# Layer 1's front split in two, its first part two images ahead, and new weights for the side work of two scan loops

## The chip, the core and the metric

The kernel runs on one core of a Trainium2 chip. The metric is the device time of one execution in microseconds, the median of several. Five engines work beside each other, each with its own queue of instructions that it takes in order: TensorE (PE in the profile, its weight loads PEld), VectorE (DVE), ScalarE (ACT), GpSimd (POOL) and SyncE (SP), which in this kernel issues all data transfers (DMA). An engine waits at the head of its queue until the semaphores of that instruction's producers are set.

## What is computed

Input x has 16 images of 192 channels and 32 x 32 pixels, in float32. Four residual blocks follow one another, each fed with a group norm (32 groups) of x:

```
x = x + layer0(gn(x))   # mLSTM block, projection, 3x3 conv, batch norm, leaky relu
x = x + layer1(gn(x))   # Mamba: layer norm, in_proj, causal conv of 4 taps, silu, scan, gate, out_proj, layer norm, proj
x = x + layer2(gn(x))   # depthwise 3x3 conv, batch norm, clip to 0..6
x = x + layer3(gn(x))   # SS2D: in_proj, depthwise 4x4 conv, four scans, layer norm, gate, out_proj, and a local branch
```

The scans of layers 1 and 3 take most of the time. For each of 384 channels and 16 states n, over 1024 positions t:

```
h[t] = exp(dt[t] * A[n]) * h[t-1] + dt[t] * x[t] * B[t, n]
y[t] = sum over n of C[t, n] * h[t]
```

Layer 1 runs one such scan per image, layer 3 four of them (rows, columns, and both reversed).

## The kernel before

**Scan steps.** Layers 1 and 2 run as one stage (`layer12`), layer 3 as another. The core of both is `scan_run` (L864 on). A step is one half image (512 positions) and one state n: 16 images x 2 halves x 16 states = 512 steps in layer 1, 4 times as many in layer 3. Channels lie in three groups t of 128 partitions. One step has

- on ACT three `xbt` (L889, u times B) and three `da` (L909, the decay exp), each a step ahead or more;
- on PE, for each group t, three transposes and a matmul into `xb` (L917, L920; 3 PSUM buffers), one step ahead, and four transposes that add h into the PSUM tile y (L951), two steps behind;
- on DVE three scan instructions (L933), which write h (4 buffers) from da (5 buffers) and xb;
- on POOL the multiplication of all of h by C (L940), on every fourth step a tile of diagonals (L899), and in the first half of an image a copy of the carried state (L939);
- on SP the broadcast of C's row (`cb`, 256 KB, 4 buffers, L891).

**Side work.** Everything else runs beside the scan, as Python generators that yield between small pieces. `Side.add(kind, steps, start, end)` gives a generator a window of steps. `Side.tick(now)` is called four times a step and advances each generator until the weight that it has yielded matches its share of the window:

```
share = self.totals.get(kind, self.total) * (now - start) / (end - start)
while now >= end or (task[4] < share and now >= task[5]):
```

The weight of a piece is what its `yield` gives (`yield 1.7`, L1224); `yield Wait(n)` holds a generator back by n steps, after a DMA was issued. The total of a kind is learned from its first task. Weights so place pieces within their window, and windows place the tasks. A scheduler of the framework then orders each engine's instructions: it keeps to this order by priority, but lets a later instruction go ahead where its engine would be free by the scheduler's own estimate. The scan's matmuls are tied to each other in order (`in_order`).

**Layer 1's tasks for image b.** `at` is 32 b. The windows in the kernel before, with the functions:

- `prep` (`scan_rows` L801, `scan_prep` L827): projections of x to dt, B and C, softplus for dt (L841 and L842 on ACT, L843 on DVE), transposes and u = dt * x (L854 to L860). `dbl` (L812) and its transposes (L819) give B as `bt` (L821). For the odd half at +1 to +13, for the next image's even half at +26 to +30.
- `layer1_gated` (L1055): the scan's sum y is transposed back (L987), D * x is added (L1063), and POOL multiplies it into the gate (L1064).
- `layer1_out` (L1228): out_proj and the skip, into `xt` (one buffer). `layer1_gate` (L1209): the gate's projection from `xn` and its silu, +8 to +12.5.
- `layer1_front` of image b + 1, +12.5 to +20: loads x and layer 0's result y0, applies layer 0's batch norm and leaky relu (L1156, L1157), adds (L1158), stores x1, group norm (`group_norm`, L321), normalises to `xf` (L1163), stores xf1, then layer norm (`layer_norm`, L349) into `xn`, and in_proj of the conv's half (L1176 on PE, L1180 on ACT), stored to `xin` in DRAM (L1181). x and `xn` are the same one-buffer tile `x1`.
- `layer1_conv` of image b + 1, +20 to +26: reads `xin` back as replicas shifted by tap (`replicas`, L1084; 6 buffers), four matmuls of 32 output columns for each tile (L1195), the bias (L1199), and silu of all of `xc` in one ACT instruction (L1206), with a table load before and one after it (L1207).
- `layer1_tail` of image b - 1, +13.5 to +25: layer norm, proj, x1 read again (L1259) and added (L1267), group norm, result padded to `xpad` (L1274) and stored.
- `layer2` of image b - 1, +25.5 to +34: replicas, depthwise conv on PE (`depthwise`, L1094), bias on ACT (L1293), bn_stats on DVE (L1295).

**Layer 3's tasks** have fixed windows in its 128 steps per image (L1359 on); their windows are not touched, only the weights that their pieces yield.

Of the kernel before, what the change touches and what calls it, by code (L numbers as in the profile page):

```python
# [10 lines left out]
F32 = mybir.dt.float32  # L11
# [8 lines left out]
HP = 96  # L20
DI = 384
S = 1024
# [229 lines left out]
class Program:  # L252
# [68 lines left out]
    def group_norm(self, pool, psum, x):  # L321

        nc = self.nc
        st = pool.tile([HP, 2, 2, 6], F32, name="gnst")
        mv = pool.tile([HP, 2, 2], F32, name="gnmv")
        for m in range(2):
            for i, h in enumerate(halves()):
                nc.vector.bn_stats(st[:, m, i], x[:, m, h])
            nc.vector.bn_aggr(mv[:, m], st[:, m].rearrange("p a b -> p (a b)"))
            yield 1  # L330
        ps = psum.tile([128, 512], F32, name="mm")
        nc.tensor.matmul(ps[:HP, :2], self.k("group", HP), mv[:, :, 0], start=True, stop=True)
        mean = pool.tile([HP, 2], F32, name="gnmean")
        nc.vector.tensor_copy(mean, ps[:HP, :2])
        d = pool.tile([HP, 2], F32, name="gnd")
        nc.vector.tensor_tensor(d, mv[:, :, 0], mean, SUB)
        q = pool.tile([HP, 2], F32, name="gnq")
        nc.vector.tensor_tensor(q, d, d, MUL)
        nc.vector.tensor_tensor(q, q, mv[:, :, 1], ADD)
        yield 1  # L340
        ps = psum.tile([128, 512], F32, name="mm")
        nc.tensor.matmul(ps[:HP, :2], self.k("group", HP), q, start=True, stop=True)
        r = pool.tile([HP, 2], F32, name="gnr")
        nc.vector.tensor_scalar(r, ps[:HP, :2], EPS, None, ADD)
        self.pow_mhalf(r)
        yield 1
        return mean, r, d

    def layer_norm(self, pool, psum, xs, outs, ones, p, n):  # L349

        nc = self.nc
# [3 lines left out]
        for x, o in zip(xs, outs):  # L355
            nc.vector.tensor_tensor(o, x, mean[:p, :n], SUB)
        yield len(xs)
        var = psum.tile([128, 512], F32, name="mm")
# [6 lines left out]
        for o in outs:  # L365
            nc.vector.tensor_tensor(o, o, var[:p, :n], MUL)
        yield len(xs)

# [432 lines left out]
    def scan_rows(self, seen, w_x, n, bp, dp, psum):  # L801
# [3 lines left out]
        nc = self.nc  # L805
# [8 lines left out]
        for q in range(n):  # L814
            nc.sync.dma_start(row[q], dbl[64 * q + RK + NS : 64 * q + XD])
        yield 2.6
        ps = psum.tile([128, 4, 128], F32, name="mm")
# [5 lines left out]
        )  # L823
        yield 0.5
        return dbl, row, bt

    def scan_prep(self, u, rows, q, xc, xt, new, w_dt, bp, psum):  # L827


        nc = self.nc  # L830
# [6 lines left out]
        for t in range(3):  # L837
# [5 lines left out]
            nc.vector.scalar_tensor_tensor(u.dt[:, t], e, 20.0, ps, MIN, MAX)  # L843
            yield 1
        u.ut = bp.tile([128, 4, DI], F32, name="ut")
        flat, xflat = u.ut.rearrange("p c d -> p (c d)"), xt.rearrange("p c d -> p (c d)")
        for j in range(3):
# [12 lines left out]
            nc.vector.tensor_tensor(flat[:, o], xflat[:, o], ps, MUL)  # L860
            yield 1.3 if new else 0.8
        u.ready = True
# [130 lines left out]
    def layer12(self):  # L993
        tc = self.tc
        with (
# [27 lines left out]
            for b in range(self.nb):  # L1023
                at = 2 * NS * b
                side.add("prep", prep(units[2 * b + 1]), at + 1, at + 13)
                if b:
                    side.add("gate", self.layer1_gated(units[2 * b - 1], bp, psum), at + 2, at + 3.5)
                    side.add("out", self.layer1_out(b - 1, bp, psum), at + 3.5, at + 8)
                side.add("silu", self.layer1_gate(b, bp, psum), at + 8, at + 12.5)
                if b + 1 < self.nb:  # L1030
                    side.add("front", self.layer1_front(b + 1, sp, bp, psum), at + 12.5, at + 20)
                if b:
                    side.add("tail", self.layer1_tail(b - 1, sp, bp, dp, psum), at + 13.5, at + 25)
                side.add("gate", self.layer1_gated(units[2 * b], bp, psum), at + 18, at + 21)
                if b + 1 < self.nb:
                    side.add("conv", self.layer1_conv(b + 1, bp, psum), at + 20, at + 26)
                if b:
                    side.add("layer 2", self.layer2(b - 1, bp, psum), at + 25.5, at + 34)
                if b + 1 < self.nb:
                    side.add("prep", prep(units[2 * b + 2]), at + 26, at + 30)  # L1040
            finish(self.layer1_front(0, sp, bp, psum))
            finish(self.layer1_conv(0, bp, psum))
            finish(prep(units[0]))
# [11 lines left out]
    def layer1_gated(self, u, bp, psum):  # L1055
# [4 lines left out]
        for t in range(3):  # L1060
# [3 lines left out]
            nc.gpsimd.tensor_tensor(im["sz"][:, t, h], im["sz"][:, t, h], o, MUL)  # L1064
            yield 1

# [21 lines left out]
    def depthwise(self, ps, blocks, reps, side):  # L1088

        width = W + side - 1  # L1090
        for r in range(side):
            for g, rep in enumerate(reps):
# [4 lines left out]
                )  # L1097
            yield 0.9

# [45 lines left out]
    def layer1_front(self, b, sp, bp, psum):  # L1145

        nc = self.nc
        x = bp.tile([HP, 2, S], F32, name="x1", bufs=1)
        nc.sync.dma_start(x, self.ins["x"][b].rearrange("(m p) t -> p m t", p=HP))
# [3 lines left out]
        for m in range(2):  # L1153
            for h in halves():
# [3 lines left out]
                nc.vector.tensor_tensor(x[:, m, h], x[:, m, h], v, ADD)  # L1158
                yield 0.5
        nc.sync.dma_start(self.x1[b], x)  # L1160
        mean, r, _ = yield from self.group_norm(sp, psum, x)
        for m in range(2):
            nc.vector.tensor_scalar(xf[:, m], x[:, m], mean[:, m : m + 1], r[:, m : m + 1], SUB, MUL)  # L1163
        nc.sync.dma_start(self.xf1[b], xf)
        yield 1
        xn = x
        for h in halves():
# [4 lines left out]
        for t in range(3):  # L1172
            for h in halves():
# [7 lines left out]
                nc.sync.dma_start(self.xin[b % 2][t][:, 3 + h.start : 3 + h.stop], o)  # L1181
                yield 1.7
        self.image[b]["xn"] = xn
# [44 lines left out]
    def layer1_out(self, b, bp, psum):  # L1228
# [6 lines left out]
        for h in halves():  # L1235
            for m in range(2):
# [7 lines left out]
                )  # L1244
                yield 2.6

    def layer1_tail(self, b, sp, bp, dp, psum):
# [3 lines left out]
        for h in halves():  # L1251
# [14 lines left out]
            for m in range(2):  # L1266
                nc.vector.scalar_tensor_tensor(  # L1267
                    x[:, m, h], ps[m][:HP], self.b_proj[:, m : m + 1], o[m][:HP], ADD, ADD
                )
            yield 3.4  # L1270
        nc.sync.dma_start(self.x2[b], x)
# [10 lines left out]
    def layer2(self, b, bp, psum):  # L1282
# [3 lines left out]
        for m in range(2):  # L1286
            for i in range(2):
# [5 lines left out]
                nc.scalar.activation(y2, ps[:HP], AF.Identity, bias=self.v96("2b", m))  # L1293
                yield 0.2
                nc.vector.bn_stats(self.stats[:, m, 2 * b + i], y2)  # L1295
                nc.sync.dma_start(self.y2[b, :, m, i * 512 : (i + 1) * 512], y2)
                yield 0.2

# [151 lines left out]
    def layer3_front(self, b, sp, bp, dp, psum):  # L1450
# [5 lines left out]
        for m in range(2):  # L1456
# [3 lines left out]
            for h in halves():  # L1460
# [3 lines left out]
                nc.vector.scalar_tensor_tensor(x[:, m, h], y2[:, h], 6.0, x[:, m, h], MIN, ADD)  # L1464
                yield 1
        mean, r, d = yield from self.group_norm(sp, psum, x)
# [10 lines left out]
    def layer3_local(self, b, sp, bp, psum):  # L1477
# [10 lines left out]
        for i, h in enumerate(halves()):  # L1488
            l = bp.tile([128, 3, 512], F32, name="tmp", bufs=1)[:HP]
            for m in range(2):  # L1490
# [6 lines left out]
                )  # L1497
                yield 0.2
            for m in range(2):
# [6 lines left out]
                nc.vector.tensor_tensor(x[:, m, h], x[:, m, h], ps[:HP], ADD)  # L1506
                yield 1.7
        nc.sync.dma_start(self.x3[b], x)
# [17 lines left out]
    def layer3_xc(self, b, bp, dp, psum):  # L1526
# [6 lines left out]
        def project(t):  # L1533
            for i in range(2):
# [9 lines left out]
                )  # L1544
                yield 1.7
            scratch[t] = dp.tile([128, (W + 3) ** 2], F32, name="xr")
# [4 lines left out]
        for t in range(3):  # L1551
            blocks = bp.tile([128, 16, 32], F32, name="taps", bufs=1)
            nc.sync.dma_start(blocks, self.t_conv[t])
            for i, h in enumerate(halves()):
# [7 lines left out]
                nc.vector.tensor_scalar(xc[:, t, h], ps, self.v128("3conv_b", t), None, ADD)  # L1562
                yield 0.2
        self.silu(xc)
        yield

    def layer3_tail(self, b, bp, psum):
# [4 lines left out]
        for i, h in enumerate(halves()):  # L1572
# [3 lines left out]
            yield from self.layer_norm(bp, psum, vs, vs, self.k("ones384"), 128, 512)  # L1576
            self.silu(sz)
            for t in range(3):
                nc.scalar.activation(
                    v[:, t, h], v[:, t, h], AF.Identity, bias=self.v128("3ln_b", t), scale=self.v128("3ln_g", t)  # L1580
                )
                yield 0.4
            nc.gpsimd.tensor_tensor(v[:, :, h], v[:, :, h], sz, MUL)
            yield 0.4
        for m in range(2):
            for h in halves():
# [8 lines left out]
                nc.sync.dma_start(self.out[b, m * HP : (m + 1) * HP, h], x)  # L1595
                yield 2.6

# [36 lines left out]
```

## Time and profile before

| | us |
|---|---|
| median of 4 runs | 17716.2 |
| the runs | 17702.94 to 17731.71 |
| the profiled execution | 17709.81 |
| its span | 17708.0 |
| layer 0 with what lies before it, to 4277 | 4277 |
| layers 1 and 2: first to last scan step, 4277 to 7835 | 3558 |
| between the two scan loops | 232 |
| layer 3's scan loop, 8067 to 17642 | 9575 |
| after the last scan | 66 |

The profile gives for each engine the time in which it was busy, by group of instructions (line of the kernel, engine, output <- inputs, shapes), the idle time in front of an instruction and what ended it (its releaser), and a timeline. Lines with L are lines of the kernel before. Records of PE overlap, since matmuls are pipelined; the time from one start to the next tells more than the record's length. The granted clock of TensorE was 0.98 of full speed in both scan loops.

### The profile page before, as it was taken

What the parts mean: (1) busy time and instruction counts of PE and PEld (TensorE: products, weight loads), DVE (VectorE), ACT (ScalarE), POOL (GpSimd) and SP (SyncE); (2) the same over time, 40 slices, a digit from 0 to 9 for tenths busy, and PEclk for the clock granted to TensorE, in tenths of its full rate; (3) what the DMA queues carried; (4) which work ended last, traced back from release to release, by engine and by line L of the source; (5) the groups of instructions that cost most, each with busy time, mean ns of one, the idle gap of its engine ahead of it and who ended that gap; (6) DMA issues with size and microseconds to landing.
All of it is one profiled execution on the core that took longest, in us unless ns stands there. A gap on an engine that the chain in (4) does not pass through costs nothing.

```text
span 17708.0 us, 263742 instructions
## 1 busy us (share of the span) xinstructions
PE 16110.7 (91%) x99836; PEld 11245.9 (64%) x99836; DVE 13340.8 (75%) x14875; ACT 11901.5 (67%) x19653; POOL 11462.2 (65%) x5556
## 2 busy tenths in 40 slices
PE   8999999898999999978999999999999999999998
PEld 4444444444655555546777777777777777777777
DVE  4454444454777777767888888888888888888888
ACT  2222222223766666656888888888888888888888
POOL 3333333333555555546887888788888888888888
PEclk8898888898999999989999999999999999999999
DMA  1111111112333333433333233333323332333232
GB/s 44 31 32 32 32 31 31 32 30 80 111 114 114 114 114 117 117 102 102 99 106 99 90 99 107 93 96 100 107 87 96 105 105 84 99 106 100 90 98 67
DMA packets 877951, 1511.10 MB, mean 85 GB/s; under 512 B 80336, under 2 KB 311197, under 8 KB 865834
## 3 DMA queue, kind: packets, MB, share of 16 engines
q1 hardware_dynamic: 876682, 1494.22, 28.7%
q8 instruction: 791, 12.96, 0.3%
q14 instruction: 478, 3.92, 0.1%
HBM read 1264.99 MB, written 228.92 MB: 84 GB/s over the span
## 4 chain that ended last, share of the span: by engine, by line
PE 30%; ACT 9%; DVE 8%; issue 4%; POOL 3%; DMA 0%; DVEq 0%; POOLq 0%; ACTq 0%; SPq 0%
PE y L951 8%; PE xb L917 7%; DVE h L933 6%; PE xb L920 4%; ACT da L909 3%; PE mm L1094 3%; ACT xbt L889 3%; POOL h L940 2%; PE mm L810 1%; PE mm L839 1%; PE mm L1517 1%; PE mm L1537 1%; PE mm L859 1%; PE mm L1502 1%; PE mm L1591 1%
## 5 line engine op out<-in xcount | busy, mean ns | idle before, releaser
L940 POOL TENSOR_TENSOR h<-h,cb 128x1536 f32<-128x1536 f32 x2560 | 8870.1, 3468 | 1427.5 <-DVE h L933 890.8
L909 ACT ACTIVATE da<-dt,neg_a 128x512 f32<-128x512 f32 x7680 | 5267.1, 714 | 1734.7 <-DVE h L933 1663.8
L933 DVE TENSOR_TENSOR_SCAN h<-da,carry,xb 128x512 f32<-128x512 f32 x3840 | 4653.5, 1263 | 662.7 <-PE xb L920 592.8
L951 PE MATMUL y<-const,h 128*128 128x128 f32 x30720 | 4720.6, 276 | 129.6 <-DVE ysum L1391 54.1
L933 DVE TENSOR_TENSOR_SCAN h<-da,xb 128x512 f32<-128x512 f32 x3840 | 4441.2, 1203 | 386.6 <-PE xb L920 275.4
L917 PE MATMUL xb<-const,xbt 128*128 128x128 f32 x23040 | 4081.2, 282 | 412.0 <-DVE h L933 254.0
L889 ACT ACTIVATE xbt<-ut,bt 128x384 f32<-128x384 f32 x7680 | 4174.1, 603 | 246.8 <-PE xb L917 245.0
L917 PEld LDWEIGHTS xb<-const,xbt 128*128 128x128 f32 x23040 | 2765.2, 143 | 1799.4 <-issue 639.2
L951 PEld LDWEIGHTS y<-const,h 128*128 128x128 f32 x30720 | 3688.2, 144 | 322.7 <-issue 265.8
L920 PE MATMUL xb<-diag,ut 128*128 128x128 f32 x15360 | 3021.2, 279 | 0.0
L920 PEld LDWEIGHTS xb<-diag,ut 128*128 128x128 f32 x15360 | 2388.8, 196 | 62.5 <-issue 62.5
L458 PE MATMUL conv<-ypad,w_conv 96*96 96x512 f32 x2304 | 1260.2, 668 | 3.1 <-ACT y L465 3.1
L939 POOL COPY carry<-h 128x3 f32<-128x3 f32 x1280 | 248.8, 194 | 1220.0 <-DVE h L933 971.4
L899 POOL TENSOR_TENSOR diag<-const,bt 128x512 f32<-128x512 f32 x640 | 680.2, 1063 | 548.3 <-PE xb L920 355.9
L753 POOL TENSOR_TENSOR hs<-h,mhm 128x384 f32<-128x384 f32 x128 | 106.3, 831 | 1032.5 <-DVE den L758 902.9
L636 POOL TENSOR_TENSOR e<-e,const 128x1536 f32<-128x1536 f32 x128 | 443.7, 3467 | 417.8 <-DMA e<-row 396.7
L458 PEld LDWEIGHTS conv<-ypad,w_conv 96*96 96x96 f32 x2304 | 381.3, 181 | 448.8 <-issue 430.3
L839 PE MATMUL mm<-dbl,w_dt 45*128 45x512 f32 x960 | 533.8, 640 | 33.9 <-DVE v L1413 16.1
L706 PEld LDWEIGHTS num<-v,p 128*128 128x128 f32 x3072 | 437.9, 220 | 71.1 <-issue 55.8
L638 ACT ACTIVATE e<-e 128x1536 f32<-128x1536 f32 x128 | 189.6, 1481 | 418.4 <-POOL e L637 387.8
L1094 PE MATMUL mm<-rep,t_dw 96*32 96x512 f32 x2304 | 433.2, 614 | 24.1 <-DMA rep<-xr 17.9
L843 DVE SCALAR_TENSOR_TENSOR dt<-lnsq,mm 128x512 f32<-128x512 f32 x480 | 322.4, 672 | 172.2 <-ACT lnsq L842 172.2
(269 smaller groups left out, 17718.6 us busy)
## 6 DMA issues: line engine op xcount, KB each, us to landing
cb<-row SPq DMA_DIRECT2D x2560, 256.0 KB
rep<-xr SPq DMA_DIRECT2D x384, 331.0 KB
e<-row SPq DMA_DIRECT2D x128, 768.0 KB
rep<-xin SPq DMA_DIRECT2D x384, 256.0 KB
rep<-xr SPq DMA_DIRECT2D x384, 228.8 KB
x<-x SPq DMA_DIRECT2D x48, 768.0 KB
xr<-xin SPq DMA_DIRECT2D x48, 612.5 KB
xr<-xpad SPq DMA_DIRECT2D x32, 867.0 KB
```

Source lines behind the costliest of these rows:

```text
L458: nc.tensor.matmul(ps[:HP], self.w_c2[:, k, t, m * HP : (m + 1) * HP], yp[:, k, r0 : r0 + 16, t % 3 : t % 3 + W], start=t + k == 0, stop=t ...
L636: nc.gpsimd.tensor_tensor(e, e, self.k0("mask")[:, None, :].to_broadcast([128, NH, 128]), ADD)
L839: nc.tensor.matmul(ps, w_dt[:, t * 128 : (t + 1) * 128], dbl, start=True, stop=True)
L889: nc.scalar.activation(t[:, c], u.ut[:, c], AF.Copy, scale=u.bt[:, c, n : n + 1])
L899: nc.gpsimd.tensor_tensor(d, ident[:, None, :].to_broadcast([128, 4, 128]), u.bt[:, 3, n : n + 4][:, :, None].to_broadcast([128, 4, 128]), ...
L909: nc.scalar.activation(da[i, t], u.dt[:, t], AF.Exp, scale=u.neg_a(t, n))
L917: in_order(nc.tensor.transpose(xb[i, t][:, c * 128 : (c + 1) * 128], xbt[i][:, c, t * 128 : (t + 1) * 128], ident))
L920: in_order(nc.tensor.matmul(xb[i, t][:, 384:], u.ut[:, 3, t * 128 : (t + 1) * 128], u.diag[n // 4][:, n % 4], start=True, stop=True, skip_ ...
L933: nc.vector.tensor_tensor_scan(hv, dv, xv, 0.0 if first else u.carry_in[:, n, t : t + 1], MUL, ADD)
L940: nc.gpsimd.tensor_tensor(h[i], h[i], u.c.pop(n)[:, None, :].to_broadcast([128, 3, 512]), MUL)
L951: in_order(nc.tensor.matmul(u.y[:, j], h[i][:, t, c * 128 : (c + 1) * 128], ident, is_transpose=True, start=n == 0 and j % 4 == 0, stop=n ...
L1094: self.nc.tensor.matmul(ps[32 * g : 32 * g + 32], blocks[:, g * side + r], seen, start=r == 0, stop=r == side - 1, skip_group_check=True,)
```

## The change

1. `layer1_front` is cut after the group norm. Its first part keeps the name and ends with `xf`, kept in SBUF; it works in the buffer `xt` instead of `x1`. The second part, `layer1_xin`, makes the layer norm and in_proj from it; only here is `x1` taken.
2. The first part runs two images ahead: for image b + 2 at steps +26.5 to +35 of image b (for image 1 at +2 to +10 of image 0). The second part runs one image ahead at +13 to +20.
3. Windows in layer 1 move: the conv from +20..26 to +18..24.5, the next even prep from +26..30 to +24.5..29.5, and others by up to 1.5 steps.
4. The weights that pieces yield are new in layers 1, 2 and 3: before they followed TensorE's work (2.6 for three matmuls of 512 columns), now the largest of the shares of TensorE, VectorE and ScalarE.

No computing instruction is added or removed. The diff without the lines that only change a weight:

```diff
             for b in range(self.nb):
                 at = 2 * NS * b
-                side.add("prep", prep(units[2 * b + 1]), at + 1, at + 13)
+                side.add("prep", prep(units[2 * b + 1]), at + 0.5, at + 12)
                 if b:
                     side.add("gate", self.layer1_gated(units[2 * b - 1], bp, psum), at + 2, at + 3.5)
                     side.add("out", self.layer1_out(b - 1, bp, psum), at + 3.5, at + 8)
-                side.add("silu", self.layer1_gate(b, bp, psum), at + 8, at + 12.5)
+                elif self.nb > 1:
+                    side.add("front", self.layer1_front(1, sp, bp, psum), 2, 10)
+                side.add("silu", self.layer1_gate(b, bp, psum), at + 8, at + 13)
                 if b + 1 < self.nb:
-                    side.add("front", self.layer1_front(b + 1, sp, bp, psum), at + 12.5, at + 20)
+                    side.add("xin", self.layer1_xin(b + 1, bp, psum), at + 13, at + 20)
                 if b:
-                    side.add("tail", self.layer1_tail(b - 1, sp, bp, dp, psum), at + 13.5, at + 25)
-                side.add("gate", self.layer1_gated(units[2 * b], bp, psum), at + 18, at + 21)
+                    side.add("tail", self.layer1_tail(b - 1, sp, bp, dp, psum), at + 14, at + 26)
+                side.add("gate", self.layer1_gated(units[2 * b], bp, psum), at + 18.5, at + 22)
                 if b + 1 < self.nb:
-                    side.add("conv", self.layer1_conv(b + 1, bp, psum), at + 20, at + 26)
+                    side.add("conv", self.layer1_conv(b + 1, bp, psum), at + 18, at + 24.5)
+                    side.add("prep", prep(units[2 * b + 2]), at + 24.5, at + 29.5)
                 if b:
-                    side.add("layer 2", self.layer2(b - 1, bp, psum), at + 25.5, at + 34)
-                if b + 1 < self.nb:
-                    side.add("prep", prep(units[2 * b + 2]), at + 26, at + 30)
+                    side.add("layer 2", self.layer2(b - 1, bp, psum), at + 26, at + 35)
+                if b + 2 < self.nb:
+                    side.add("front", self.layer1_front(b + 2, sp, bp, psum), at + 26.5, at + 35)
             finish(self.layer1_front(0, sp, bp, psum))
+            finish(self.layer1_xin(0, bp, psum))
             finish(self.layer1_conv(0, bp, psum))
...
     def layer1_front(self, b, sp, bp, psum):
...
-        x = bp.tile([HP, 2, S], F32, name="x1", bufs=1)
+        x = bp.tile([HP, 2, S], F32, name="xt", bufs=1)
...
         nc.sync.dma_start(self.xf1[b], xf)
+        self.image[b]["xf"] = xf
         yield 1
-        xn = x
+
+    def layer1_xin(self, b, bp, psum):
+
+        nc = self.nc
+        xf = self.image[b].pop("xf")
+        xn = bp.tile([HP, 2, S], F32, name="x1", bufs=1)
         for h in halves():
             yield from self.layer_norm(
```

The weights, old to new, by function:

| function | pieces and their weights |
|---|---|
| group_norm | 1, 1, 1 (and 1 for the second half's statistics) to 0.7, 0.7, 0.5, 0.5 |
| layer_norm, m tiles | m, m to 0.3 m, 0.6 m |
| scan_rows | 2.6, 0.5 to 0.9, 0.2 |
| scan_prep | dt 1 to 0.9; u 1.3 (0.8 where x is not new) to 0.45 (0.35) |
| depthwise, a row of taps | 0.9 to 0.3 |
| layer1_gated | 1 to 0.6 |
| layer1_front's add; in_proj | 0.5 to 0.6; 1.7 to 0.6 |
| layer1_out; layer1_tail's proj | 2.6 to 0.9; 3.4 to 1.1 |
| layer2, bias; statistics | 0.2, 0.2 to 0.4, 0.3 |
| layer3_front's add | 1 to 0.7 |
| layer3_local: after the conv; pointwise | 0.2 to 0.4; 1.7 to 0.8 |
| layer3_xc: projection; bias | 1.7 to 0.8; 0.2 to 0.4 |
| layer3_tail | a new 1.5 after the silu; 0.4, 0.4 to 0.5, 1; out_proj 2.6 to 0.9 |

## The prediction

> **What bounds the kernel now.** I read the busy line first, then the busy time by stage, then what VectorE (DVE) waits for, then single lumps in order of time.
>
> ```profile
> PE 16110.7 (91%) x99836; PEld 11245.9 (64%) x99836; DVE 13340.8 (75%) x14875; ACT 11901.5 (67%) x19653; POOL 11462.2 (65%) x5556
> ```
>
> PE looks like the bound at 91%, but its records overlap: 4 of the y matmuls fill 0.60 us while the next instruction starts 0.44 us after the first. So a transpose costs 0.11 us, not the 276 ns of its record, and the 24 of one scan step 2.6 us. The stages (columns: stretch, length, then busy us of PE, PEld, DVE, ACT, POOL, clock, DMA share, GB/s):
>
> ```profile
> 4277.00:7835.00 3558.00, 3211.61 (x19133) 2120.14 (x19131) 2729.90 (x2957) 2466.51 (x3940) 2090.97 (x1017) 0.98 0.38 114
> 8067.00:17642.00 9575.00, 8903.97 (x65174) 7095.16 (x65173) 8506.40 (x8137) 8213.38 (x13929) 7888.30 (x3626) 0.98 0.32 97
> ```
>
> ```profile
> 5368.10:5595.00 226.90, 204.76 (x1219) 133.09 (x1219) 174.77 (x192) 157.03 (x251) 131.61 (x65) 0.98 0.39 117
> ```
>
> The first row is layer 1 and 2 (512 steps, 6.95 us each), the second layer 3 (2048 steps, 4.68 us each), the third one image of layer 1 (32 steps). A step without side work takes 3.33 us, three scans at 1.11 us from start to start. So DVE sets the pace: a step's time is DVE's work plus DVE's idle time. Idle are 828 us (23%) in layer 1 and 1069 us (11%) in layer 3. The change leaves DVE's instructions as they are, so only the idle time and the lengthening of single instructions can move. DVE's idle time in layer 1, 4700 to 7300 us, which is 2600 / 226.9 = 11.46 images (us in total, times, longest):
>
> ```profile
> DVE h L933 <- PE xb L920: 148.9, 188, 2.6
> DVE dt L843 <- ACT lnsq L842: 81.0, 47, 2.0
> DVE bt L821 <- PE mm L819: 47.1, 9, 5.6
> ...
> DVE xt L1267 <- DMA o<-x1d: 27.7, 11, 3.4
> DVE xc L1199 <- PE mm L1195: 27.4, 10, 5.7
> ...
> DVE x L1158 <- DMA x<-x: 14.9, 12, 1.5
> ```
>
> and in layer 3, 8100 to 17600 us (15.9 images of about 600 us):
>
> ```profile
> DVE h L933 <- PE xb L920: 660.1, 534, 8.1
> DVE h L933 <- ACT da L909: 95.7, 138, 5.0
> DVE dt L843 <- ACT lnsq L842: 59.4, 73, 1.8
> ```
>
> In layer 1 about two thirds of the idle time comes at side instructions, which stand in DVE's queue before their producer is done, with the scans behind them. In layer 3 it comes mostly at the scans. Lumps of image 5 in order of time (start, us, what, idle before and releaser):
>
> ```profile
> 5450.80 5.23 DVE L1158 TENSOR_TENSOR x<-x,xf 96x512 f32<-96x512 f32 x4 [1.24 <-DMA x<-x]
> ...
> 5566.77 0.23 DVE L821 COPY bt<-mm 128x64 f32<-128x64 f32 x1 [5.20 <-PE mm L819]
> ```
>
> The first is the old front (residual adds, then 4 bn_stats): 9 us of DVE without a scan. The second is the copy of B, which waits for a projection whose ACT part came behind the conv's Silu.
>
> **The method.** The listings of both programs show each engine's order. I count places in steps by each engine's own recurring instructions (TensorE and ScalarE work for the step ahead) and call *lead* the steps by which a producer stands before its reader. Each reader's wait in the trace, by its lead, prices its lead in the new listing. Every line keeps its number of instructions, but for two more ACT table loads.
>
> **Layer 1, per image.**
> - dt L843, 7.1 us now (81.0 / 11.46): three of six readers have lead -0.67 and wait 2.1 us each, those at 0 about 0.4. New leads: one at -0.67, two at -0.33 (between the two prices, 1.4 taken), three positive. 2.1 + 2.8 + 0.4 = 5.3: **-1.8**.
> - bt L821, 4.1 to 4.4 us now. The conv's Silu with its two table loads (1.28 + 2.77 + 1.28 us on ACT) moves from step 26 to 24, and bt is read at 26, not 27. I price it at the 0.9 of the leads that remain: **-3.5**.
> - Residual add L1158 waits 14.9 / 11.46 = 1.3 us for x's load. It is now issued at step 24, two steps before the add: **-1.3**.
> - Reuse of the o tiles behind xin's stores -0.8; L1157 behind L1156 -0.7; second layer norm step (L366) and small ones -0.7: **-2.2**.
> - xc L1199: the conv now starts at step 18, before xin ends at 20. Two of its first eight replica loads stand on SP behind the last store to xin, whose ACT instruction is at 20.3, while TensorE wants them at 19.9. The worse lead priced as above: **+2.8**.
> - The reload L1267 is met by three waits, not two (+1.6); ut L860 (+0.5) and xpad L1274 (+0.7) lose lead: **+2.8**.
>
> Together -8.8 + 5.6 = -3.2 us. Two more terms. L1158 ran as four in a row; the new listing has three, a scan, and one more.
>
> ```profile
> L1158 DVE TENSOR_TENSOR x<-x,xf x48: 674/677/3800, 4771.2 to 7281.8; 96x512 f32<-96x512 f32 x48
> ```
>
> At 62.8 us for 48 the mean is 1.31 us, so a run of four loses some 2.6 us, nearly all on its first: such an add can last as long as a POOL multiplication of h (3.47 us). A second run costs 0 to 3.1 us (3.80 - 0.67); POOL is busy 58% of the image, so I take half the length times that, **+1.0**. The Trainium skill (SBUF — State Buffer, Terms) says that VectorE and GpSimd share a port pair, held for a whole instruction, and that the loser fully blocks; that speaks against bringing such adds near scans. By it all four adds and both normalisations L1163 could each wait a full 3.47 us, 21 us per image; the 677 ns median says that most do not.
>
> And TensorE stood 5.4 us per image at the group norm's matmul (61.9 us waiting for L329) and 2.1 at the layer norm's (24.1 for L1163). Both inputs now come steps earlier. But the scans of steps 13 to 17 waited only 1.4 us per image: this is all it can give, **-1.4**.
>
> Sum -3.6 us for 15 images: **-54 us**. What moves without cost: the front's 4 large transfers on SP (x and y0 in, x1 and xf1 out, 768 KB each) go to steps 15, 24, 27 and 33, among layer 2's replica loads. The DMA engines are 58% busy in image 5's steps 22 to 31, and 2.3 MB more beside the 12 MB there is about 69%; without that cover the 256 KB broadcast of C (cb) would come late and POOL would wait. The weights within tasks add nothing: they only place.
>
> **Layer 3.** The same tasks in the same windows; only the spacing moves. dt +1.7, xt L1594 -1.3, ut -0.1: +0.3 us an image, 16 images, **+5**. Two table loads at 1.28: **+3**.
>
> Against the profiled execution (17709.8 us, span 17708.0): -54 + 5 + 3 = -46, 17664. It lies 6 us under the median of the four, 17716.2, so I say **17670**. What stays unpriced is the scans' wait for TensorE (13.0 us per image in layer 1, 41 in layer 3): the listings do not tell it. A quarter either way is 13.0 x 15 / 4 = 49 and 41 x 16 / 4 = 164, together 213 us: 17457 to 17883.
>
> **Rivals.**
> - *Lumps meet within one step* (slower). Largest of the sums of PE, DVE and ACT in each step, every instruction at its start-to-start time: mean 5.82 before, 5.91 after in layer 1; 4.61 and 4.63 in layer 3. The new peaks: Silu and layer norm on ACT at step 13 (11.3 us), DVE 9.3 at 17 (the next front's L1157 beside the tail), ACT 10.2 at 24. If the buffers (3 xb, 5 da) do not bridge a step, the time follows these sums: 1.4% of 3558 = 51 and 0.35% of 9575 = 34, so 17709.8 + 85, **17795**. It decides when the lag between ACT and DVE exceeds one step; averaged over two steps the sums are 5.45 and 5.42 in layer 1, 4.38 and 4.40 in layer 3. For it: sums explain most of a step's time. Against: ACT peaks of 10 us exist now, and at step 14 of layer 3's image DVE barely idles.
> - *The scans' wait goes too* (much faster). If TensorE, no longer held at the front, halves the 13.0 us and takes a tenth of layer 3's 41: 17664 - 98 - 66, **17500**. Against: TensorE's hold lay beside a DVE lump.
> - *Nothing to measure.* The change does only half of what it says: in the new listing the front's L1156 and L1157 climb back to steps 17 and 18 as soon as xf is free, into the dense stretch. Gains and losses then cancel: **17710**.
>
> **Numbers.** Small gain 0.36, much faster 0.12, nothing 0.17, slower 0.35. A measurement of this kernel tells about 0.2% (35 us) from no change. Faster 0.48, same 0.17, slower 0.35. The range takes the unpriced quarter: 17460 to 17880.
>
> **What will show it.** DVE idle at bt L821 near 1 us per image and at dt L843 near 5; no wait of L1158 for x; TensorE's wait at L332 for the front gone; more waiting at xc L1199 and a wait of TensorE for rep<-xin. Layer 1's stage near 3505 us, layer 3's within 10 us of 9575. If layer 3 moves by more than 50 us, the spacing matters in a way that I did not price; if layer 1 grows while these waits fall, the rival of the lumps is right.

## The result, and the profile after

| | before | changed |
|---|---|---|
| median | 17714.8 us (53 runs) | 17732.2 us (33 runs) |
| ratio to before, 95% interval | | 1.0009 (1.0004 to 1.0013) |
| profiled execution, its span | 17709.81, 17708.0 us | 17705.36, 17703.6 us |
| layers 1 and 2, first to last scan step | 3557.5 us | 3526.7 us |
| layer 3's scan loop | 9574.3 us | 9601.8 us |

The forecast was 17670 us, a gain of 0.26%. Measured is a loss of 0.04 to 0.13% by the interval, so no change by the forecast's own bound of 0.2%. The two profiled executions show a gain of 31 us in layer 1 and a loss of 27 us in layer 3. The profiled execution of the changed kernel lies 27 us under its median, that of before 5 us under its own, so the two profiles flatter the change.

Lines are now those of the changed kernel. After L1028 they stand higher than before: L1158 is now L1162, L1163 L1167, L1195 L1205, L1199 L1209, L1259 L1269, L1267 L1277, L1562 L1572, L1594 L1605. The stages of the changed kernel (stretch, length, busy us of PE, PEld, DVE, ACT, POOL, clock, DMA share, GB/s):

```profile
4275.90:7802.60 3526.70, 3233.78 (x19118) 2140.16 (x19116) 2681.46 (x2946) 2451.09 (x3939) 2078.18 (x1016) 0.96 0.39 114
8036.20:17638.00 9601.80, 8890.34 (x65171) 7112.33 (x65169) 8475.24 (x8137) 8206.12 (x13930) 7877.38 (x3626) 0.97 0.32 97
```

What VectorE waits for in the changed kernel, layer 1, 4700 to 7300 us (us in total, times, longest):

```profile
DVE h L933 <- PE xb L920: 182.3, 184, 2.8
DVE xt L1277 <- DMA o<-x1d: 80.3, 25, 6.7
...
DVE xc L1209 <- PE mm L1205: 43.0, 33, 1.5
...
DVE dt L843 <- ACT lnsq L842: 25.8, 24, 1.9
```

The same of the changed kernel in layer 3, 8100 to 17500 us:

```profile
DVE h L933 <- PE xb L920: 639.1, 527, 6.5
DVE xc L1572 <- PE mm L1098: 100.6, 61, 7.9
DVE dt L843 <- ACT lnsq L842: 89.4, 88, 2.0
...
DVE xt L1605 <- PE mm L1602: 56.9, 30, 3.8
```

and two rows of the kernel before for the same stretch, which the forecast didn't list:

```profile
DVE xt L1594 <- PE mm L1591: 28.0, 31, 1.5
DVE xc L1562 <- PE mm L1094: 10.5, 30, 2.7
```

Against the rows of before: bt L821 (47.1) is gone, dt fell from 81.0 to 25.8, and the residual add waits 2.6 for x's load (14.9 before). In their place the addition of the reloaded x1 (27.7 to 80.3), the scans (148.9 to 182.3) and the conv's bias (27.4 to 43.0) wait longer. In layer 3 dt (59.4 to 89.4) and xt (28.0 to 56.9) rose, and VectorE, which waited 10.5 us at the bias of the depthwise conv, waits 100.6 there.

### The profile page after: what moved, and what is told of

Same layout as the page of the kernel before. It is cut to its first block, busy times and chain, and to the rows that moved or that the text cites. A ratio compares the mean times of both kernels' runs of the same rounds, so it can differ in the third digit from the quotient of the medians.

```text
span 17703.6 us, 263677 instructions
## 1 busy us (share of the span) xinstructions
PE 16093.8 (91%) x99836; PEld 11270.1 (64%) x99836; DVE 13267.7 (75%) x14875; ACT 11878.9 (67%) x19655; POOL 11442.1 (65%) x5556
## 5 line engine op out<-in xcount | busy, mean ns | idle before, releaser
L839 PE MATMUL mm<-dbl,w_dt 45*128 45x512 f32 x960 | 547.3, 654 | 48.2 <-DVE v L1423 24.5
L1098 PE MATMUL mm<-rep,taps 128*32 128x512 f32 x3072 | 412.5, 605 | 24.9 <-DMA rep<-xr 18.0
```

The lines of the kernel that those rows point to most:

```text
L839: nc.tensor.matmul(ps, w_dt[:, t * 128 : (t + 1) * 128], dbl, start=True, stop=True)
L1098: self.nc.tensor.matmul(ps[32 * g : 32 * g + 32], blocks[:, g * side + r], seen, start=r == 0, stop=r == side - 1, skip_group_check=True,)
```

## The experiments

Each ratio is to the kernel before on the same chip. Beside it stand the lengths of layer 1's stage and layer 3's loop in the run's own profile, and they show where the time went: the stretch ahead of layer 1, which has the same order of instructions in the changed kernel and in w1_gate_out, took 4276 us in the one and 4324 in the other. A stage is read from a single profile, and two profiles of one order differ by up to 19 us in layer 1; where the ratio says something else, it decides.

**Which part of the change does what.** Four kernels undo or do one part:

- l3_old: all of the change, but layer 3's weights as before.
- l3_alone: the kernel before, with layer 3's new weights.
- l1_split: the split front and the new windows, all weights as before.
- l1_weights: the kernel before, with the new weights of layers 1 and 2.

In functions that both layers call, a flag that layer 3 sets picks the weight, here in l3_old:

```diff
-            yield 0.3
+            yield (0.9) if self.third else (0.3)
```

> The changed kernel, but every weight that layer 3's tasks yield as before (so layer 1 has the split, the new windows and the new weights; layer 3 is the layer 3 of before). Theory A, the two stages are separate and layer 3's new weights cost what its scan loop lost in the profiles: layer 1's stage near 3527 us as in the changed kernel, layer 3's scan loop near 9574 as before, time 17715 - 31 = 17684, faster than before by 0.17%. Theory B, the +27 us of layer 3's loop (and the -31 of layer 1's) are what two executions of one kernel differ by: the loop anywhere between 9570 and 9605 and the time near the changed kernel's 17732. Theory C, the stages are coupled (layer 1's new order changes what layer 3 finds): layer 3's loop stays near 9600 with the old weights.

> The kernel before with layer 3's new weights alone; layer 1 is unchanged. Theory A: layer 1's stage 3558, layer 3's loop 9602, time 17715 + 27 = 17742, and VectorE waits some 90 us at the bias of layer 3's conv (L1562) for the depthwise matmuls, where it waited 10.5. Theory B (difference of executions): 17715, even if that wait is there. The prediction's own step for layer 3 was +5 to +8: 17722.

> The split front and the new windows of layer 1 with the old weights everywhere; layer 3 is as before. If the split and the windows make layer 1's gain, as the prediction said (weights only place): layer 1's stage near 3527, time 17684, copy of B (L821) without wait. If the weights make it: stage 3550 to 3558, time 17707 to 17715. With the prediction's sum of -54: 3504 and 17661.

> The kernel before (front in one piece, old windows) with layer 1's and layer 2's new weights alone; layer 3 as before. If the split and the windows make the gain: stage 3553 to 3563, time 17710 to 17720. If the weights make it: near 3527 and 17684. If the weights by themselves are the part that costs (pieces pushed together, the scans waiting more for TensorE): stage 3575 or more and 17732.

| kernel | ratio, 95% interval | layer 1 | layer 3 |
|---|---|---|---|
| l3_old | 0.9983 (0.9974 to 0.9992) | 3546.1 | 9560.0 |
| l3_alone | 1.0031 (1.0019 to 1.0042) | 3571.7 | 9615.5 |
| l1_split | 0.9969 (0.9957 to 0.9981) | 3499.3 | 9558.8 |
| l1_weights | 1.0023 (1.0014 to 1.0031) | 3602.2 | 9564.3 |

Theory A holds, B and C fall: the stages are separate, and layer 3's new weights cost some 40 us whatever layer 1 does. The split and its windows alone gain 55 us by the ratio, as much as forecast; all the new weights together then cost, in both layers. The windows of l1_split:

```profile
4282.50:7781.80 3499.30, 3179.19 (x19115) 2130.60 (x19114) 2731.77 (x2946) 2453.26 (x3939) 2078.24 (x1016) 0.97 0.40 115
8014.10:17572.90 9558.80, 8885.78 (x65171) 7072.24 (x65169) 8502.82 (x8137) 8212.11 (x13929) 7888.26 (x3626) 0.98 0.32 97
```

**Which of layer 1's weights.** On l1_split, the new weights of some tasks only: in w1_xin_tail those of layer1_xin and layer1_tail with the norms that they call, in w1_prep_l2 those of the preps, layer 2 and layer1_front with its group norm. For instance:

```diff
 w1_xin_tail, layer1_tail:
-            yield 3.4
+            yield 1.1
 w1_prep_l2, scan_rows:
-        yield 2.6
+        yield (2.6) if self.third else (0.9)
```

> The split kernel with all weights old (l1_split: layer 1's stage 3499 us, 0.9969 of before), and the new weights only in the second part of the front (layer1_xin) and in the tail, with the layer norms and group norm that they call. Theory W1, the weights cost where they push the pieces of xin and tail together in the dense steps 13 to 26: nearly all of the 47 us that the new weights cost in layer 1 (3499 to 3546) are here: stage near 3540, ratio 0.999; waits at the reload (L1277), the bias of the conv (L1209) and the gate (L1067) come back. Theory W2, the cost is spread over all tasks or sits in prep and layer 2: stage 3499 to 3520, ratio 0.997 to 0.998.

> The same split kernel with the new weights only in the preps, layer 2 and the first part of the front. Theory W1: stage 3499 to 3506, ratio 0.997, since dt's and u's waits fall as the new weights spread dt and the scans' wait grows by as much. Theory W2: stage 3520 to 3546, ratio 0.998 to 0.999. If the two halves together cost far more or far less than 47 us, the pieces of different tasks meet and the cost is not a sum by task.

Measured: w1_xin_tail 0.9942 (0.9928 to 0.9955), layer 1 3464.9; w1_prep_l2 0.9949 (0.9936 to 0.9961), 3458.1. Both halves gain 34 to 41 us where together, in l3_old, they seemed to cost 47. W1 and W2 fall alike. Two weights were in neither half, those of the gate and of out. In these tasks all pieces weigh the same, so their spacing should not depend on the weight:

```diff
 w1_gate_out = l1_split with
-            yield 1      (layer1_gated, three pieces)
+            yield 0.6
-                yield 2.6    (layer1_out, four pieces)
+                yield 0.9
```

w1_rest is l1_split with all new weights of layer 1 but these two.

> The split kernel with all weights old (layer 1's stage 3499 us), but layer1_gated's pieces weigh 0.6 instead of 1 and layer1_out's 0.9 instead of 2.6. In both tasks all pieces weigh the same, so the spacing within the window is the same by intent; only the rounding of the comparison of weight with share moves a piece by one tick, a quarter of a step. Theory S (spacing): nothing moves, stage 3490 to 3508, ratio 0.9967. Theory Q (what counts is which pieces of different tasks meet within a quarter step): the stage moves by 20 us or more either way.

> The split kernel with all of layer 1's new weights except these two; layer 3 as before. It holds both halves whose runs gave 3465 (xin and tail) and 3458 (preps, layer 2, first part of the front). If parts add up: 3499 - 34 - 41 = 3424, ratio 0.993 or less, and the loss of l3_old (3546) came from the gate's and out's quarter steps. If the two halves collide with each other: 3530 to 3560, ratio 0.998, and w1_gate_out stays at 3499. In between, 3450 to 3500: neither.

Measured: w1_gate_out 1.0000 (0.9991 to 1.0009), layer 1 3589.7; w1_rest 0.9937 (0.9925 to 0.9950), 3452.3, so the halves together gain 47 us and not the 75 of their sum. Two weights that were to do nothing cost 90 us on l1_split and 94 on w1_rest by the stages (l3_old is w1_rest with them). By the ratios they cost 55 (0.0031) and 81 (0.0046). The profiled execution of w1_gate_out lies 41 us above the median of its eleven and that of l1_split 39 us under the median of its six, so the 90 is too large and the 55 the better figure. Given back in the changed kernel:

```diff
 after_gate = the changed kernel with
-            yield 0.6
+            yield 1
-                yield 0.9
+                yield 2.6
```

> The changed kernel with two weights as before: layer1_gated 1 and layer1_out 2.6. If these two made the loss in layer 1 in the changed kernel too: stage from 3527 to 3450 to 3470, layer 3's loop 9602, time 17732 - 65 = 17667, ratio to before 0.997. If the loss needs more than these two: stage 3500 or more, ratio 0.999 to 1.001.

Measured: 0.9962 (0.9948 to 0.9975), layer 1 3450.5, as expected: 76 us less by the stage, 83 by the ratio. The windows of after_gate:

```profile
4284.30:7734.80 3450.50, 3204.00 (x19118) 2119.20 (x19116) 2665.64 (x2946) 2460.24 (x3939) 2081.43 (x1016) 0.97 0.39 117
7972.70:17580.20 9607.50, 8890.68 (x65171) 7108.13 (x65169) 8473.58 (x8137) 8206.09 (x13931) 7876.30 (x3626) 0.97 0.31 97
```

**How two weights move anything.** The total that a task learns is not the sum of its weights but the sum plus 1 (`self.totals[kind] = task[4] + 1`, L222). So weights have a scale: three pieces of 1 start at 0, 1/4 and 1/2 of the window, three of 0.6 at 0, 0.6/2.8 and 1.2/2.8. With the gate's window of 3.5 steps and ticks at .0, .3, .6 and .9 of a step, its second piece goes from 19.6 to 19.3; out's third and fourth go one tick earlier as well.

Which of the two costs, the traces tell by the steps of the image (images 2 to 15 together, from the starts of the scans). w1_gate_out is 80 us longer than l1_split in steps 18 to 27, and 4 us in steps 0 to 17. l3_old is 126 us longer than w1_rest in steps 18 to 27 and the changed kernel 116 us longer than after_gate; in the other steps they are shorter, by 31 and 45. So the loss stands in the gate's second window, +18.5 to +22, and behind it, and not in out's, +3.5 to +8.

What the gate's tick does is seen on SyncE's queue. Steps 19 to 21 of one image, first in the changed kernel (start, us, DMA issues):

```profile
5731.37 0.32 SPq L891 DMA_DIRECT2D cb<-row  x1
5731.78 0.38 SPq L1191 DMA_DIRECT2D xin<-o  x1
5732.26 1.83 SPq L1088 DMA_DIRECT2D rep<-xin  x3
5735.97 0.80 SPq L1269 DMA_DIRECT2D o<-x1d  x2
```

then in after_gate:

```profile
5706.59 0.32 SPq L1269 DMA_DIRECT2D o<-x1d  x1
5708.01 0.32 SPq L1191 DMA_DIRECT2D xin<-o  x1
5708.72 1.82 SPq L1088 DMA_DIRECT2D rep<-xin  x3
5710.63 0.53 SPq L1269 DMA_DIRECT2D o<-x1d  x1
5711.21 0.51 SPq L1088 DMA_DIRECT2D rep<-xin  x1
5711.78 0.58 SPq L891 DMA_DIRECT2D cb<-row  x1
```

In after_gate both reloads stand ahead of the cb load, in the changed kernel behind it (so it is in all of images 3 to 15). There this cb load waited, by what SyncE's queue waits for between 5722 and 5737 us:

```profile
SPq L891 <- POOL h L940: 8.7, 1, 8.7
SPq L1269 <- DMA xin<-o: 1.7, 1, 1.7
```

Counted from the start of step 19 (5718.52 and 5696.85) the reloads go out at 17.4 us (one right after the other) in the changed kernel, at 9.7 and 13.8 in after_gate. On VectorE the changed kernel shows

```profile
5732.05 0.72 DVE L1067 SCALAR_TENSOR_TENSOR o<-xc,p,mm 128x512 f32<-128x512 f32 x1
5732.69 1.28 DVE L933 TENSOR_TENSOR_SCAN h<-da,carry,xb 128x512 f32<-128x512 f32 x1
5739.45 1.40 DVE L1277 SCALAR_TENSOR_TENSOR xt<-mm,b_proj,o 96x512 f32<-96x512 f32 x2 [5.49 <-DMA o<-x1d]
```

and after_gate

```profile
5713.23 0.75 DVE L1277 SCALAR_TENSOR_TENSOR xt<-mm,b_proj,o 96x512 f32<-96x512 f32 x1 [1.27 <-PE mm L1273]
...
5716.07 0.75 DVE L1277 SCALAR_TENSOR_TENSOR xt<-mm,b_proj,o 96x512 f32<-96x512 f32 x1 [1.38 <-DMA o<-x1d]
5716.74 0.73 DVE L1067 SCALAR_TENSOR_TENSOR o<-xc,p,mm 128x512 f32<-128x512 f32 x1
```

The gate's second addition stands ahead of the reload's in the one and behind it in the other; the gate writes, and the reload fills, tiles of the same two buffers `o`. Over layer 1's stage VectorE idles 107 us at L1277 in the changed kernel and 56 in after_gate (sums of the trace's idle times before the line within the stage; the expectations count up to 12 us more at a line). Of the 60 us that it idles more in all (845 and 785), 51 so stand at the reload.

**Is it the waiting cb load?** Two kernels, both with the slow order of w1_gate_out, and a control for the first:

```diff
 gate_cb5 (on w1_gate_out), split_cb5 (on l1_split):
-  ... name="cb", bufs=4)
+  ... name="cb", bufs=4 if self.third else 5)
-        st = pool.tile(..., name="gnst")
+        st = pool.tile(..., name="gnst", bufs=1)
 gate_cbpool (on w1_gate_out):
-            nc.sync.dma_start(c_n, ...)
+            (nc.sync if self.third else nc.gpsimd).dma_start(c_n, ...)
```

> w1_gate_out (layer 1's stage 3590) with five buffers instead of four for the broadcast row of C, cb, in layer 1 (and one instead of two for the group norm's statistics, for room). The order on SyncE's queue is that of w1_gate_out. Theory H, the cb trigger that waits for GpSimd holds up the reload of x1 and the replica loads behind it: with a free buffer it no longer waits, VectorE's idle time at L1277 and L1209 (102 and 66 us) falls to that of l1_split (85 and 19) or below, stage 3490 to 3510, ratio 0.997. Rival G, the cost is where the gate's additions stand on VectorE and GpSimd: stage stays at 3570 or more, ratio 1.000.

> l1_split (3499) with the same fifth cb buffer: the control. Theory H: its cb triggers stand behind the reload already, so it gains less than gate_cb5: 3470 to 3499, ratio 0.995 to 0.997, and the two kernels come within 15 us of each other. Rival G: it gains as much as gate_cb5 does, or neither gains.

> w1_gate_out (layer 1's stage 3590) with layer 1's loads of cb triggered from GpSimd's queue, right behind the multiplication that frees their buffer, instead of from SyncE's; VectorE's order is nearly the same. Theory H (the waiting cb trigger blocks SyncE's queue ahead of the reload and the replicas): idle time of VectorE at L1277 falls from 102 us to 85 or less and at L1209 from 66 to 20 or so, and the stage to 3500 or less, if the 512 triggers cost GpSimd little. Rival G (where the gate's additions stand on VectorE): L1209 and L1277 keep 60 and 100 us. If the triggers themselves slow GpSimd, the scans show it instead and the stage tells nothing; the two idle times still do.

Measured: gate_cb5 1.0004 (0.9996 to 1.0013), layer 1 3561.6; split_cb5 0.9968 (0.9957 to 0.9979), 3515.8. This pair decides nothing, because the edit did not take the wait away. SyncE's queue in gate_cb5, 4700 to 7300 us (w1_gate_out had 1458.1):

```profile
SPq L891 <- POOL h L940: 1460.4, 317, 7.7
```

With a free buffer the load is queued one step earlier, and stands and waits there: the trigger for step n goes out in step n - 4 in 420 of 512 cases, in w1_gate_out in step n - 3 in 427. gate_cbpool: 0.9980 (0.9972 to 0.9989), layer 1 3535.1, 55 us less by the stage and 35 by the ratio. VectorE's waits in w1_gate_out

```profile
DVE xt L1277 <- DMA o<-x1d: 67.8, 24, 3.9
DVE xc L1209 <- PE mm L1205: 48.1, 36, 2.0
```

and in gate_cbpool

```profile
DVE xc L1209 <- PE mm L1205: 55.1, 39, 2.2
DVE xt L1277 <- DMA o<-x1d: 33.8, 25, 3.1
```

and in l1_split

```profile
DVE xt L1277 <- DMA o<-x1d: 55.2, 36, 3.1
DVE xc L1209 <- PE mm L1205: 5.7, 16, 1.4
```

The reload's wait goes with the cb load, as theory H said; the conv's bias keeps its wait, as rival G said. But this is not the loss taken back. In steps 20 to 23 of images 2 to 15, w1_gate_out is 71 us longer than l1_split and gate_cbpool 75. What gate_cbpool gains, it gains in step 18, where it is 42 us shorter than l1_split and w1_gate_out only 8 us longer; VectorE's idle time at the reload there is 14 us, against 44 and 43 in the other two. So the cb load that waits cost time at a reload that the two weights had not touched, and that it makes the loss of w1_gate_out is not shown. l1_split with cb on GpSimd's queue, which would tell, was not run.

What the traces do show: of the 85 us that VectorE idles more in w1_gate_out than in l1_split, 45 stand at the conv's bias, 21 at the scans and 19 at the reload, while in the changed kernel against after_gate the reload has 51 of 60. The same two weights cost at different readers in the two kernels. In the changed kernel the order of the triggers is seen in the trace, but no run moved them alone. Why the conv's matmuls come later for the bias in w1_gate_out is not settled.

**The reload's buffers.** On l1_split, three buffers for `o` in place of two, then together with each half of the weights:

```diff
-  bp.tile([128, 512], F32, name="o")
+  bp.tile([128, 512], F32, name="o", bufs=3)
```

The group norm's statistics have one buffer for it, as above. best_a has the weights of w1_xin_tail too, best_b those of w1_prep_l2.

> The split kernel with old weights, with three buffers instead of two for the tile o, into which the tail reloads x1 (and one instead of two for the group norm's statistics, to make room). In the split kernel VectorE idles 85 us at the addition of the reload (L1277), whose transfer starts only when an older store from o has landed. Theory O: this wait falls below 30 us and half of what it frees reaches the stage: 3499 to 3470, ratio 0.9953. Rival: the wait moves to the scans or to the conv of the same steps, stage 3490 to 3500, ratio 0.9968.

> The split kernel, new weights in xin and tail alone, three buffers for o; layer 3 as before. If the gains of w1_xin_tail (3465) and of o3 (3471) against 3499 add up: 3437, ratio 0.9925. If they are the same wait (reload L1277 and what follows): 3460, ratio 0.994. By theory Q no sum holds: anywhere from 3430 to 3510.

> The split kernel, new weights in preps, layer 2 and the first part of the front alone, three buffers for o; layer 3 as before. If the gains add up (3458 and 3471 against 3499): 3430, ratio 0.9925. If not: 3450 to 3510.

Measured: o3 0.9941 (0.9929 to 0.9954), layer 1 3470.6. The idle time at L1277 within the stage falls from 73 to 44 us, and with it the stage by the same 29 us: the wait stays above theory O's 30, the stage comes out as it said. best_a 0.9912 (0.9898 to 0.9926), 3429.1, and best_b 0.9922 (0.9910 to 0.9934), 3434.1: here the gains do add (3437 and 3430 were the sums). best_a, median 17592 us beside 17743 for the kernel before, is the fastest version found.

**Layer 3.** On l1_split, parts of layer 3's new weights: in w3_prep_tail those of the preps and the tail (with layer_norm), in w3_xc_local those of the conv, the local branch and the front (with depthwise and group_norm), in w3_rows all but one:

```diff
 w3_rows, depthwise (against the changed kernel):
-            yield 0.3
+            yield 0.9
```

> The split kernel with old weights in layer 1 and layer 3's new weights, except that a row of depthwise taps keeps its 0.9. Theory D, the weight of 0.3 lets the four rows of taps of layer 3's conv be issued within one step and so costs the 42 us of layer 3's loop: the wait of VectorE at the bias L1572 falls from 100 to some 15 us, the loop to 9565, ratio 0.9972. Theory E, the loop loses by the whole of the new spacing (dt, the tail's out_proj, v, the local branch): the wait at L1572 goes but the loop stays at 9590 to 9610, ratio 0.999.

> l1_split (layer 3's loop 9559) with layer 3's new weights in the preps and the tail alone (with layer_norm). If the cost of layer 3's new weights (9602, +42) is a sum by task, the waits at dt (+31), the tail's xt (+30) and u (-24) belong here and the scans at step 25 move to step 28: 9565 to 9580. If parts don't add, anything from 9540 to 9650.

> l1_split with layer 3's new weights in the conv's task, the local branch and the front alone (with group_norm and depthwise). If the cost is a sum by task, the wait at the conv's bias (+92) belongs here, some of it taken from the scans: 9580 to 9600. The two halves together should then give 42 us; if they give far less or more, they collide or relieve each other.

| kernel | ratio, 95% interval | layer 3 |
|---|---|---|
| w3_rows | 1.0041 (1.0029 to 1.0054) | 9703.2 |
| w3_prep_tail | 0.9988 (0.9979 to 0.9996) | 9600.7 |
| w3_xc_local | 0.9976 (0.9966 to 0.9985) | 9588.5 |

With all old weights the loop took 9557 to 9578 us in 14 profiles (median 9565), with all new ones 9602, 9607 and 9616. The halves cost 36 and 24, 60 together, against 42: nearly a sum. D fell beyond E: keeping 0.9 removes the wait at the bias (102 us of idle time to 4), yet the loop is 100 us longer than in the changed kernel, and TensorE now waits for the replica loads, for which it waited 2.8 us in the changed kernel. TensorE's waits in w3_rows, 8100 to 17500 us:

```profile
PE mm L1098 <- DMA rep<-xr: 45.0, 31, 5.0
```

and VectorE's scans wait 212 us more, 7.8 us per image of it in step 82. A single weight put back is not the old spacing: the share of its task is a new one. Why layer 3's new spacing as a whole costs is told here by where VectorE waits, and no run isolates one cause.

## Why the prediction failed

The step that failed is one sentence: "The weights within tasks add nothing: they only place." Placing moves time: the weights shifted both layers, down and up, by amounts as large as the whole forecast gain. Each of the orders below was profiled at least twice in layer 1, and so a budget can be made of the means:

| | layer 1's stage | step |
|---|---|---|
| order of before (before, l3_alone: 3557.5, 3571.7) | 3564.6 | |
| split and windows, old weights (l1_split and the three of layer 3: 3499.3, 3506.0, 3503.4, 3505.8) | 3503.6 | -61 |
| and new weights but gate and out (w1_rest, after_gate: 3452.3, 3450.5) | 3451.4 | -52 |
| and those two (changed, l3_old: 3526.7, 3546.1) | 3536.4 | +85 |

With layer 3's 9607 against 9565, +42, the sum is +14 us; the medians differ by 17.4. The ratios of the runs give the same four steps as -55, -57, +81 and +46.

- *What bounds the kernel.* Held in its sum: the time goes by VectorE's work and idle time. But the length of its instructions moves more than the +1.0 an image that was allowed for it. The -52 us of the second step are shorter instructions: VectorE's busy time in the stage is 2731.8 us in l1_split and 2665.6 in after_gate, its idle time 767 and 785.
- *Layer 1, -54.* In l1_split it came out at -55 us by the ratio and -58 to -61 by the stage, but not by its terms, so that the match is partly luck. Idle us per image there against forecast (the stage's change over 15 images): bt -4.1 (-3.5), L1158's wait -1.1 (-1.3) and reload +1.7 (+1.6) came near, but dt -5.0 (-1.8), xc -1.6 (+2.8), ut -1.8 (+0.5), the gate -3.4 and out +2.1 (no term) did not. All side instructions together waited 12.1 us less, where -3.2 were forecast, and the scans' wait, which the sum left out but for -1.4, took most of the surplus: +8.1 us per image (231 to 352 us in the stage).
- *The scans' wait, a quarter either way.* Set too small in layer 1: it rose by half in l1_split. In the changed kernel layer 3's fell, from 819 to 710 us of idle time, while the waits at xc, dt and xt rose by 90, 30 and 29. In both layers a wait that went at one reader came back in part at others.
- *TensorE's hold at L332.* Gone, as forecast, with nothing for the scans.
- *The extra run of L1158 on the shared port, +1.0.* Too large, and in the wrong place: the mean of the line went from 1.39 to 1.42 us in l1_split, 0.1 us an image. What grew is a far smaller instruction, the group norm's L338 (38 to 77 us in the stage; told below), while the normalisation to `xpad` fell from 58 to 24. In the second step L338 falls to 7 us and L1162, the old L1158, from 79 to 47, but L339 behind L338 rises from 5 to 40: part of the wait only moved on by one instruction.
- *Reload +1.6.* Right in l1_split (+1.7), too small in the changed kernel (+4.0): the method counted the reload's waits, and had nothing for a cb load that waits ahead of it on SyncE's queue.
- *Layer 3, +5.* +42. Per image, in the two profiles, dt came as forecast (+1.9 for +1.7), xt with the wrong sign (+1.8 for -1.3), and xc, the largest with +5.6, had no term. The scans' wait gave 6.8 back, and VectorE's busy time 31 us in all.
- *The rivals.* "Nothing to measure" came out, 17710 for 17732, but not by its mechanism: l1_split has the climb of L1156 and L1157 to steps 17 and 18 and gains 55 us. The slower rival (lumps within one step) would have lost time in layer 1 through its new windows, which gained.

The forecast had a sign for this case: "If layer 3 moves by more than 50 us, the spacing matters in a way that I did not price." Layer 3 moved by 27 us in the two profiles and by 42 in the medians of the loops, so the sign did not show, though the spacing mattered; layer 1 moved by more, both ways.

## What to carry to other kernels

Where pieces of side work are placed by weights, read how the weights become places, down to the constant that is added: here a scale that should cancel moved a piece by one tick, and by the ratios that was worth 55 to 83 us of 3500. Look then at what changed places, on the issuing queue too, where a transfer's trigger that waits can come to stand ahead of another; a fifth buffer did not help here, since the trigger was only queued earlier. Check by steps, too, that a remedy gains where the loss was: here one gave more than half of the loss back, but in another step. And when one edit carries a structure and many numbers, undo each group by itself: the same structure gave -55 us alone and +17 with its numbers, and -0.9% with a better choice of them and a third buffer.

## What the runs showed of the hardware

- A transfer's trigger that waits holds the triggers behind it on its engine's queue: 8.7 us in one image above. With the 256 KB cb loads issued by GpSimd (592 ns of its time for each), VectorE's wait for the reload fell from 67.8 to 33.8 us, and the stage became 55 us shorter in the profile, the kernel 35 us by the ratio. The Trainium skill (DMA: Bandwidth & Descriptors, Issuing engines are not separate DMA queues) says that issuing from several engines saves only the time to initiate a transfer. Here it saved a wait as well, and the measurement decides.
- An instruction of 2 elements per partition, the group norm's L338 (4700 to 7300 us), took 3332 ns in the median in l1_split and 127 ns in w1_rest, whose order differs. One of them in l1_split, and the GpSimd multiplication of h beside it:

```profile
5802.48 3.37 DVE L338 TENSOR_TENSOR gnq<-gnd 96x2 f32<-96x2 f32 x1
5802.39 3.44 POOL L940 TENSOR_TENSOR h<-h,cb 128x1536 f32<-128x1536 f32 x1
```

Of the 30 in l1_split's stage 27 take more than 1 us, and each of these ends 13 to 18 ns after a multiplication that had begun before it. Over layer 1 the line's busy time is 77 us in l1_split and 7 in w1_rest, where 11 of 30 L339 are held in the same way: what a small instruction costs here hangs on what GpSimd does beside it, not on its size.
- The stretch ahead of layer 1, with the same instructions in the same order, took 4276 us at a granted clock of 0.88 in the changed kernel and 4324 at 0.87 in w1_gate_out. A change in the scan loops is therefore better read from their own stretch.
